# Layer 1 of a four-layer sequence model: attention weights turned by VectorE in 32x32 blocks, and weighed in array tiles of 32 rows by 64 columns

## The chip, the cores and the metric

The kernel runs on one core of a Trainium2 chip. The metric is device microseconds for one execution of the program, lower is better. Durations inside an execution come from one execution that the hardware profiler recorded; its times count from the first recorded instruction (the span).

## What is computed

Four layers act in turn on x, 8 sequences of 512 positions with 256 features, all in float32. Layers 0, 1 and 2 are transformer blocks (normalization, modulation by a condition vector, attention, a two-layer perceptron). Layer 3 is a bidirectional state-space layer. The change is in the attention of layer 1, which has 16 heads of 64 features:

```python
q, k, v = split(modulate(layernorm(x)) @ W_qkv)          # 16 heads of 64
attn = softmax(einsum('bqhd,bkhd->bhqk', q, k) * 64 ** -0.5)
out = einsum('bhqk,bkhd->bqhd', attn, v).reshape(B, T, 1024)
x = x + g_msa * (out @ W_out + b_out)
```

Layers 0 and 2 have 16 heads of 16 features. They form the transposed scores directly, so that their weights need no transposing.

## The kernel before, in words

**Layout and stages.** Activations lie with features on the partitions and the 512 positions along the free dimension. The three transformer layers are one program part: its list `units` holds one unit per batch for layers 0 and 2, and two per batch for layer 1 (`Cfg`, line 62; a unit is 8 heads), hence 8 + 16 + 8 units. The recurrence of layer 3 follows, in pools of its own. Its `fill` (line 1271) is of use here for its matmuls: 64 rows by 32 columns of the array, eight such tiles at a time, 128 moving columns each.

**Who sets the order.** All engines are on a manual schedule: each engine's instructions stand in the order in which the Python code emits them, and an engine starts an instruction only when all earlier ones on it have started. DMAs stand in order in SP's queue. Attention of layer 1 is `attend_q` (line 486). Its loop (line 548) runs over rounds. A round is two items of 128 queries for two heads, so four score tiles of 128 queries by 512 keys, and layer 1 has 128 rounds. In round r it emits:

1. `scores` of round r (line 494): four matmuls, two heads side by side in 64 rows of the array each, into four PSUM banks.
2. `weights` of round r (line 504): per tile a row maximum on VectorE (510) and an exponential on ScalarE that also sums its rows (511).
3. `weigh` of round r-2 (line 532): 16 matmuls of 128 columns, V as the stationary operand (128 keys by 64 features), two heads side by side in 64 columns of the array each; after four items a ScalarE copy of the finished output (545).
4. a share of the dense work (`dense.products`, line 333).
5. `turned` of round r-1 (line 522): per tile four TensorE transposes of 128x128 into a PSUM bank (529) and a VectorE copy of the bank to SBUF (530).
6. `divide` of round r (line 516): a reciprocal on VectorE (518) and one multiplication per tile on GpSimd (520).
7. a second share of dense work.

**Dense work.** `prep` (line 386) makes a unit's normalized input, Q, K and V, and must be done before the unit's first scores (`prepared`, 342). It waits in emission until the unit two before has been scored and weighed. `post` (line 680) makes the output projection and the perceptron of a batch. `products` hands out this work at `Q_RATE` units per round, in pieces that are not split, and lets a round go without when earlier pieces ran over. So the rounds are uneven: a piece can be 8 matmuls of 512 columns.

**Buffers.** PSUM has eight banks. Seven form a ring from which `bank()` (line 125) takes the next one; the eighth holds the output that `weigh` accumulates. The exponentials lie in four buffers of tag `p`, two rounds' worth. float32 matmuls appear in the profile as two records each (two passes), a transpose as one.

Of the kernel before, what the change touches and what calls it, by code (L numbers as in the profile page):

```python
# [7 lines left out]
F32 = mybir.dt.float32  # L8
# [10 lines left out]

LEAD, K_RATE, Q_RATE = 6, 3.7, 6.0  # L20
GELU = 4.0
# [27 lines left out]
class Cfg:  # L49
# [12 lines left out]
    Cfg(0, 16, 32, 1, 1e-5, AF.Gelu, (2, 0, None, 6, 4, None)),  # L62
    Cfg(1, 64, 64, 2, 1e-5, AF.Gelu, (0, 2, 4, 6, 8, 10)),
    Cfg(2, 16, 32, 1, 1e-6, AF.Gelu_apprx_tanh, (0, 2, 4, 6, 8, 10)),
# [10 lines left out]
def dit_mamba_kernel(ctx: ExitStack, tc: tile.TileContext, t, out):  # L75
# [44 lines left out]
    with ExitStack() as actx:  # L120
        apool = actx.enter_context(tc.tile_pool(name="apool", bufs=1))
        a2 = actx.enter_context(tc.tile_pool(name="a2", bufs=2))
        ps = actx.enter_context(tc.tile_pool(name="ps", bufs=1, space=PSUM))

        def bank():
            return ps.tile([128, L], F32, tag="s", name="s", bufs=7)

# [74 lines left out]
        def load_attn(cfg, g=0):  # L202
            l = cfg.layer
            src = t[f"wqkv{l}"].rearrange("(k p) m -> p k m", p=128)
            w = apool.tile([128, 2, 1536 if l == 1 else 768], F32, tag="wqkv", name="wqkv")
            if l == 1:

                for i in range(3):
                    o = i * 1024 + g * 512
                    nc.sync.dma_start(w[:, :, i * 512 : (i + 1) * 512], src[:, :, o : o + 512])  # L210
            else:
                for i in range(2):
                    pad = a2.tile([128, 2, L], F32, tag="p", name="pad", bufs=N_P)
                    nc.sync.dma_start(pad, src[:, :, i * 512 : (i + 1) * 512])
                    for k in range(2):
                        dst = w[:, k, i * 256 : (i + 1) * 256].rearrange("p (h r) -> p h r", r=16)
                        nc.gpsimd.tensor_copy(dst, real(pad[:, k, :]))
                nc.sync.dma_start(w[:, :, 512:768], src[:, :, 1024:1280])
                bv = apool.tile([128, D], F32, tag="bv", name="bv")
                nc.sync.dma_start(bv, t[f"bv{l}"].to_broadcast([128, D]))  # L220
                W["bv"] = bv
            W["qkv"] = w
# [55 lines left out]

        negp = [apool.tile([128, 4, 128], F32, tag=f"negp{i}", name="negp") for i in range(2)]
        clear(0, nc.vector)  # L280
        for i in range(2):
            nc.gpsimd.memset(negp[i], 0.0)
        load_x(0, 1)
        load_out(CFGS[0])

        class Unit:


            def __init__(self, idx, cfg, b, g):
                self.idx, self.cfg, self.b, self.g = idx, cfg, b, g  # L290
                self.i2 = idx % 2
                self.first = b == 0 and g == 0
                self.last = b == B - 1 and g == cfg.n_groups - 1
                self.ready = self.scored = self.weighed = False
                self.ot = {}
                self.qT, self.kT = qts[self.i2], kts[self.i2]
                self.v = vt[self.i2].rearrange("p (t h d) -> p t h d", t=4, d=cfg.pad)

# [87 lines left out]
        def prep(u):  # L386

            cfg, b, l = u.cfg, u.b, u.cfg.layer
            before = units[u.idx - 2] if u.idx > 1 else None
            load_x(l, b)  # L390
            if (l == 1 or u.first) and u.idx:
# [13 lines left out]
            if l == 1:  # L405
                for c in range(4):
                    p = plain(w, c * 128, h, 2)
                    nc.vector.tensor_scalar(u.qT[:, c, :], p, cfg.qscale, None, ALU.mult)
                    yield DONE
                    p = plain(w, 512 + c * 128, h, 2)  # L410
                    nc.scalar.copy(u.kT[:, c, :], p)
                    yield DONE
                while not before.weighed:
                    yield PASS
                for tt in range(4):
                    p = bank()
                    for k in range(2):
                        nc.tensor.matmul(
                            p, h[:, k, tt * 128 : (tt + 1) * 128], w[:, k, 1024:1536], start=k == 0, stop=k == 1
                        )  # L420
                    nc.scalar.copy(u.v[:, tt, :, :], p.rearrange("p (h d) -> p h d", d=64))
                    yield DONE
                u.ready = True
                return
            if l == 2:
                if b < 2:
                    while not before.weighed:
                        yield PASS
                    clear(u.i2, nc.gpsimd)
# [19 lines left out]
            for k in range(2):  # L449
# [12 lines left out]
                yield DONE  # L462
            while before and not before.weighed:
                yield PASS
# [21 lines left out]
        def attend_q(us):  # L486


            cfg = us[0].cfg
            nh = cfg.nh  # L490
            rounds = [(u, i) for u in us for i in range(0, 16, 2)]
            pr, pt, o = {}, {}, {}

# [10 lines left out]
            def weights(u, it, ss):  # L504
                c, qt = divmod(it, 4)
                p = pr[u, it] = a2.tile([128, 2, L], F32, tag="p", name="pr", bufs=N_P)
# [15 lines left out]
            def turned(u, it):  # L522
                d = pt[u, it] = [a2.tile([128, L], F32, tag=tag, name="pt") for tag in ("q2", "qks")]
                p = pr.pop((u, it))
                for j in range(2):
                    tp = bank()
                    for kt in range(4):
                        sl = slice(kt * 128, (kt + 1) * 128)
                        nc.tensor.transpose(tp[:, sl], p[:, j, sl], ident)  # L529
                    nc.vector.tensor_copy(d[j], tp)  # L530

            def weigh(u, it):
                c, qt = divmod(it, 4)
                if qt == 0:
                    o[c] = ps.tile([128, L], F32, tag="o", name="o")
                p = pt.pop((u, it))
                for kt in range(4):
                    for j in range(2):
                        nc.tensor.matmul(
                            o[c][rows(cfg, j), qt * 128 : (qt + 1) * 128], u.v[:, kt, c * 2 + j, :],  # L540
                            p[j][:, kt * 128 : (kt + 1) * 128], start=kt == 0, stop=kt == 3,
                        )
                if qt == 3:
                    u.ot[c] = out_tile()
                    nc.scalar.copy(u.ot[c], o[c])
                    u.weighed = c == 3

            for r in range(len(rounds) + 2):
                pend = []
                if r < len(rounds):  # L550
                    u, i = rounds[r]
                    if i == 0:
                        dense.prepared(u)
                    ss = [scores(u, i + k) for k in range(2)]
                    u.scored = i == 14
                    pend = [(u, i + k, weights(u, i + k, ss[k])) for k in range(2)]
                if r >= 2:
                    u, i = rounds[r - 2]
                    for k in range(2):
                        weigh(u, i + k)  # L560
                dense.products(Q_RATE / 2, 6, 2)
                if 1 <= r <= len(rounds):
                    u, i = rounds[r - 1]
                    for k in range(2):
                        turned(u, i + k)
                for args in pend:
                    divide(*args)
                dense.products(Q_RATE / 2, 6, 2)

        def attend_k(us):  # L570
# [26 lines left out]
            def extend(u, c):  # L597
                p = bank()
                for qt in range(4):
                    nc.tensor.transpose(p[:, qt * 128 : (qt + 1) * 128], negp[c % 2][:, qt, :], ident)  # L600
                q2[u, c] = a2.tile([128, L], F32, tag="q2", name="q2")
                nc.vector.tensor_tensor(q2[u, c], u.qT[:, c, :], p, ALU.add)

            def weigh(u, c, kt, pt):
                if kt == 0:
                    o[c] = ps.tile([128, L], F32, tag="o", name="o")
                for j in range(4):
# [9 lines left out]
                if c == 0:  # L617
                    u.s16 = a2.tile([16, L], F32, tag="s16", name="s16")
                if c % 2 == 0:
# [60 lines left out]
        def post(us):  # L680
# [9 lines left out]
            if l != 1:  # L690
# [3 lines left out]
                for qt in range(4):  # L694
                    nc.tensor.transpose(
                        p[:, qt * 16 : (qt + 1) * 16], u.s16[:, qt * 128 : (qt + 1) * 128], ident[0:16, 0:16]
                    )
                rec = a2.tile([128, 64], F32, tag="rec", name="rec")
                nc.vector.reciprocal(rec, p[:, 0:64])  # L699
                wide = apool.tile([128, 64, 16], F32, tag="wide", name="wide")  # L700
                nc.gpsimd.tensor_copy(wide, rec[:, :, None].to_broadcast([128, 64, 16]))  # L701
# [3 lines left out]
                for k in range(2):  # L705
                    p = bank()
                    for qt in range(4):
                        nc.tensor.transpose(
                            p[:, qt * 128 : (qt + 1) * 128], wide[:, qt, k * 128 : (k + 1) * 128], ident
                        )  # L710
                    nc.vector.tensor_tensor(u.ot[k], u.ot[k], p, ALU.mult)
                    yield 1
                yield PASS
# [853 lines left out]
```

## Time and profile before

| what | value |
| --- | --- |
| timed runs | 6252.9, 6258.54, 6271.06 us; median 6258.54 us |
| span of the profiled execution | 6255.0 us, mean granted clock 0.970; a time of its own besides the span is not recorded |
| layer 1's attention | first score matmul at 915.4 us, last weigh matmul ends at 2456.7 us |
| TensorE busy over the whole span | 5768.5 us (92%) |
| VectorE, ScalarE, GpSimd busy over the whole span | 4102.2, 3549.7, 3674.4 us |
| DMA | 260.34 MB, mean 42 GB/s |

The profile is read by stage: the shares of the whole span mix the attention layers with the recurrence, whose limits are others. "PE" is TensorE's matmuls, "PEld" its weight loads, "DVE" VectorE, "ACT" ScalarE, "POOL" GpSimd. In a group's row, busy is the time in which at least one of the group's instructions ran, and the mean is that of one instruction. Matmuls overlap, so that a matmul's mean is far longer than the distance from one start to the next. A merged row of the timeline gives a start, a length and a count: the length less one matmul's own duration, over the count less one, is that distance.

### The profile page before, as it was taken

To read this page: it belongs to the slowest core of one execution; us is meant where nothing else is said; L and a number is where in the kernel's file an instruction comes from. 1 tells how busy PE (TensorE), PEld (TensorE's weight loads), DVE (VectorE), ACT (ScalarE), POOL (GpSimd) and SP (SyncE) were. 2 spreads that over 40 slices of the span, in tenths; PEclk is the share of its full clock that TensorE was granted. 3 is DMA by queue.
4 is the path that set the end of the run, shared out by engine and by line. 5 is a ranking of instruction groups with operands and counts; after the bars stand their busy time and mean duration, and the time that the engine had idled before them with its cause. 6 is when DMAs were issued, how large, how long until landed. Compare 5 with 4: busy or idle time off the path is not lost. (4 is left out here: it accounts for less than half of the span.)

```text
span 6255.0 us, 200766 instructions
## 1 busy us (share of the span) xinstructions
PE 5768.5 (92%) x88988; PEld 2903.6 (46%) x88988; DVE 4102.2 (66%) x5109; ACT 3549.7 (57%) x6854; POOL 3674.4 (59%) x1467
## 2 busy tenths in 40 slices
PE   9999999999999998999998788898898988888887
PEld 4333335555555554333333444554455545444544
DVE  4555445444455544454552599888889888888887
ACT  2444443333344333344443677878777778777784
POOL 2010026555566565111110499999999989999897
PEclk8999999999999999999998899999999999999999
DMA  2000100000000000101000211212121111212120
GB/s 89 25 24 25 36 23 31 31 28 18 28 27 12 28 27 15 45 20 31 23 17 11 73 53 49 73 53 70 54 60 53 59 59 55 67 57 67 54 66 26
DMA packets 168913, 260.34 MB, mean 42 GB/s; under 512 B 40544, under 2 KB 58976, under 8 KB 168048
## 3 DMA queue, kind: packets, MB, share of 16 engines
q1 hardware_dynamic: 166992, 245.92, 12.9%
q8 instruction: 703, 11.52, 0.8%
q10 hardware_dynamic: 1056, 1.57, 0.1%
q14 instruction: 162, 1.33, 0.1%
HBM read 186.53 MB, written 34.60 MB: 35 GB/s over the span
## 5 line engine op out<-in xcount | busy, mean ns | idle before, releaser
L1297 POOL TENSOR_TENSOR hs<-hs,cs 128x2048 f32<-128x2048 f32 x512 | 2324.3, 4573 | 205.3 <-DVE hs L1293 131.8
L1293 DVE TENSOR_TENSOR_SCAN hs<-da,bx 128x512 f32<-128x512 f32 x2048 | 2303.0, 1197 | 201.8 <-PE bx L1279 130.7
L1254 ACT ACTIVATE da<-dtr,negA 128x512 f32<-128x512 f32 x2048 | 1394.5, 716 | 482.8 <-DVE hs L1293 471.4
L1279 PE MATMUL bx<-dg,ut 64*32 64x128 f32 x65536 | 1111.0, 273 | 183.5 <-DVE hs L1293 104.8
L1279 PEld LDWEIGHTS bx<-dg,ut 64*32 64x32 f32 x65536 | 925.3, 106 | 592.2 <-issue 449.7
L520 POOL TENSOR_SCALAR pr<-pr,sums 128x512 f32<-128x512 f32 x512 | 796.9, 1574 | 572.4 <-DVE sums L518 572.0
L593 DVE TENSOR_REDUCE negp<-s 128x1 f32<-128x512 f32 x1024 | 637.6, 683 | 590.4 <-PE s L588 590.0
L644 ACT ACTIVATE pt<-s 128x512 f32<-128x512 f32 x1024 | 528.0, 602 | 442.1 <-PE s L638 442.0
L1325 PE MATMUL yc<-hs,r 128*32 128x512 f32 x4096 | 573.7, 615 | 39.9 <-POOL hs L1297 39.8
L511 ACT ACTIVATE pr<-s,negm 128x512 f32<-128x512 f32 x512 | 345.1, 686 | 298.7 <-DVE negm L510 285.0
L530 DVE COPY pt<-s 128x512 f32<-128x512 f32 x512 | 322.0, 683 | 193.5 <-PE s L529 179.8
L510 DVE TENSOR_REDUCE negm<-s 128x1 f32<-128x512 f32 x512 | 317.3, 682 | 142.1 <-PE s L499 142.0
L588 PE MATMUL s<-kT,qT 32*128 32x512 f32 x2048 | 368.1, 654 | 36.2 <-ACT pt L644 18.2
L353 POOL TENSOR_TENSOR xs<-x 128x512 f32<-128x512 f32 x48 | 61.0, 1272 | 566.3 <-DVE x L664 187.4
L675 PE MATMUL s<-g,w_w 128*128 128x512 f32 x768 | 368.6, 627 | 23.9 <-ACT g L739 14.6
L1227 ACT ACTIVATE dg<-eye,bt 128x64 f32<-128x64 f32 x1528 | 381.5, 343 | 1.1 <-PE bx L1279 1.0
L701 POOL COPY wide<-rec 128x1024 f32<-128x1024 f32 x16 | 16.6, 1037 | 622.1 <-DVE rec L699 622.1
L381 PE MATMUL s<-h,w_w 128*128 128x512 f32 x768 | 364.0, 615 | 12.3 <-POOL h L372 12.3
L381 PE MATMUL s<-h,wqkv 128*128 128x512 f32 x768 | 366.1, 611 | 5.1 <-POOL h L372 5.1
L638 PE MATMUL s<-q,kT 32*128 32x512 f32 x2048 | 365.8, 649 | 1.9 <-DVE qs L455 1.4
L529 PE MATMUL s<-base,pr 128*128 128x128 f32 x2048 | 266.1, 281 | 43.6 <-POOL pr L520 38.5
L1325 PEld LDWEIGHTS yc<-hs,r 128*32 128x32 f32 x4096 | 122.6, 110 | 392.5 <-issue 261.2
(191 smaller groups left out, 6250.6 us busy)
## 6 DMA issues: line engine op xcount, KB each, us to landing
dtr<-dt_s SPq DMA_DIRECT2D x1024, 64.0 KB
cs<-c_s SPq DMA_DIRECT2D x256, 128.0 KB
wqkv<-in_wqkv_dram SPq DMA_DIRECT2D x48, 512.0 KB
dt_s<-dt SPq DMA_DIRECT2D x15, 1024.0 KB
x_mid<-x SPq DMA_DIRECT2D x24, 512.0 KB
x<-x_mid SPq DMA_DIRECT2D x24, 512.0 KB
ot<-ot SPq DMA_DIRECT2D x256, 32.0 KB
w<-in_w_in_dram SPq DMA_DIRECT2D x16, 512.0 KB
```

The source lines that it names most:

```text
L381: nc.tensor.matmul(p, w[:, k, o : o + 128], src[:, k, :], start=k == 0, stop=k == n - 1)
L520: nc.gpsimd.tensor_scalar(p[:, j, :], p[:, j, :], sums[:, j : j + 1], None, ALU.mult)
L588: nc.tensor.matmul(ss[j], u.qT[r, c, qt * 128 : (qt + 1) * 128], u.kT[r, c, :], start=True, stop=True)
L593: nc.vector.tensor_reduce(negp[c % 2][:, qt, i : i + 1], ss[j], AX.X, ALU.max, negate=True)
L644: nc.scalar.activation(pt[j // 2][:, j % 2, :], ss[j], AF.Exp)
L675: nc.tensor.matmul(p, w[:, first + c, m * 128 : (m + 1) * 128], srcs[c], start=c == 0, stop=c == n - 1)
L1227: nc.scalar.activation(o[:, n, :, i], eye, AF.Copy, scale=bt[:, 4 * i + n : 4 * i + n + 1])
L1254: nc.scalar.activation(da[:, i, :], dtr[step, 4 * c + j], AF.Exp, scale=negA[:, 4 * c + j, g : g + 1])
L1279: nc.tensor.matmul(bx[k][32 * n : 32 * n + 32, r, 128 * s : 128 * s + 128], uts[c][64 * r : 64 * r + 64, s, 32 * j : 32 * j + 32], d[64 * ...
L1293: nc.vector.tensor_tensor_scan(h, back(da[:, i, :]), back(x[:, i, :]), 0.0, ALU.mult, ALU.add)
L1297: nc.gpsimd.tensor_tensor(hs[t_], hs[t_], cs[step, k % 16 // 4][:, None, :, :].to_broadcast([128, 2, 2, L]), ALU.mult,)
L1325: nc.tensor.matmul(yc[c][32 * j : 32 * j + 32, :], r32, h[j // 2][:, j % 2, i, :], start=False, stop=gp == n_p - 1 and i == 1, tile_positi ...
```

## The change

Layer 1 is split into four units per batch, of four heads each (so 32 units), with `Q_RATE` 6.4 for 6.0. Its weights are turned in blocks of 32x32 on VectorE, straight from SBUF to SBUF. A block transpose of a tile of 128 queries by 512 keys leaves 32 keys on the partitions for each of the four groups of 32 queries, so each group of 32 partitions needs V of all keys. V is therefore written to DRAM once per unit, and read back four times, once into each group of 32 partitions. `weigh` then runs once for two heads and all 512 queries (64 times in all, in the odd rounds), as 128 matmuls of 32 rows by 64 columns with 128 moving columns, in eight array tiles, into four PSUM banks. All eight banks are now one ring (`s8`), from which `weigh` takes four neighbouring ones: the next four, or banks 0 to 3 if the next four would run over the end. Per unit two Q and two K products of 512 columns remain, and V is made in pieces of 256 columns. The buffers of the turned weights and of V's copies lie in Q, K and V tiles that layers 0 and 2 use; so at the turn to layer 2 its first unit waits, in emission, until layer 1's last unit has been scored, and clears its tiles on GpSimd after that. The turned weights' second pair of buffers waits for the division in the last batch of layer 0.

```diff
-LEAD, K_RATE, Q_RATE = 6, 3.7, 6.0
+LEAD, K_RATE, Q_RATE = 6, 3.7, 6.4
...
-    Cfg(1, 64, 64, 2, 1e-5, AF.Gelu, (0, 2, 4, 6, 8, 10)),
+    Cfg(1, 64, 64, 4, 1e-5, AF.Gelu, (0, 2, 4, 6, 8, 10)),
...
+        s8 = ps.tile([128, 8, L], F32, tag="s", name="s")
+        ring, n_ring = [0], [7]
         def bank():
-            return ps.tile([128, L], F32, tag="s", name="s", bufs=7)
+            i = ring[0] % n_ring[0]
+            ring[0] = i + 1
+            return s8[:, i, :]
+        def four_banks():
+            i = ring[0] % n_ring[0]
+            i = i if i <= 4 else 0
+            ring[0] = i + 4
+            return s8[:, i : i + 4, 0:128]
...
+        turned_t = [t_.rearrange("p (b q) -> p b q", q=128) for t_ in (extra, vt[1], aux, work)]
+        spread_t = [
+            t_.rearrange("p c t -> p (c t)").rearrange("p (b d) -> p b d", d=128) for t_ in (qts[1], kts[1])
+        ]
+        v_dram = [dram.tile([L, 256], F32, tag=f"vd{i}", name="v_dram") for i in range(2)]
...
+                nc.sync.dma_start(v_dram[u.i2].rearrange("(t p) d -> p t d", p=128), u.v)
                 u.ready = True
...
+            def spread_v():
+                while waiting and len(spread) < 2 and waiting[0][0].ready:
+                    u, c = waiting.pop(0)
+                    t_ = spread[u, c] = spread_t[c]
+                    for a in range(4):
+                        nc.sync.dma_start(
+                            t_[32 * a : 32 * a + 32, :, :],
+                            v_dram[u.i2][:, 128 * c : 128 * c + 128].rearrange("(b i) d -> i b d", i=32),
+                        )
...
             def turned(u, it):
-                d = pt[u, it] = [a2.tile([128, L], F32, tag=tag, name="pt") for tag in ("q2", "qks")]
+                c, qt = divmod(it, 4)
+                if qt == 0:
+                    heads[u, c] = [turned_t[(turns[0] + j) % 4] for j in range(2)]
+                    turns[0] += 2
+                    while turns[0] == 4 and not units[u.idx - 1].divided:
+                        dense.step(dense.posts)
                 p = pr.pop((u, it))
                 for j in range(2):
-                    tp = bank()
-                    for kt in range(4):
-                        sl = slice(kt * 128, (kt + 1) * 128)
-                        nc.tensor.transpose(tp[:, sl], p[:, j, sl], ident)
-                    nc.vector.tensor_copy(d[j], tp)
...
+                    nc.vector.transpose(heads[u, c][j][:, :, qt * 32 : qt * 32 + 32], p[:, j, :])
+            def weigh(u, c):
+                p, v, o = heads.pop((u, c)), spread[u, c], four_banks()
+                for b in range(16):
+                    for a in range(4):
+                        r = slice(32 * a, 32 * a + 32)
+                        for j in range(2):
+                            d = slice(64 * j, 64 * j + 64)
+                            nc.tensor.matmul(
+                                o[d, a, :], v[r, b, d], p[j][r, b, :], start=b == 0, stop=b == 15,
+                                tile_position=(32 * a, 64 * j),
+                            )
+                spread.pop((u, c))
...
```

## The prediction

> **What bounds the kernel now.** I read the table by stretch first, for the stage that the change touches: from the first score matmul of layer 1 to its last weigh.
>
> ```profile
> core 0: us, PE busy (x) PEld busy (x) DVE busy (x) ACT busy (x) POOL busy (x), PEclk, DMA share, GB/s
> 915.00:2457.00 1542.00, 1471.92 (x8799) 842.49 (x8796) 778.78 (x1450) 596.26 (x1352) 918.82 (x609) 0.97 0.07 25
> ```
>
> PE is busy 1472 of 1542 us; DVE 51%, ACT 39%, POOL 60%, DMA 7%. So PE's work sets the stage, 12.0 us for each of 128 rounds. Next the waits of PE in the same stretch, for the 70 us that are left, and the groups:
>
> ```profile
> PE s L529 <- POOL pr L520: 38.5, 49, 1.5
> PE s L675 <- DVE qs L455: 9.2, 1, 9.2
> ...
> PE s L529 <- ACT pr L511: 4.8, 3, 2.2
> ```
>
> ```profile
> L520 POOL TENSOR_SCALAR pr<-pr,sums 128x512 f32<-128x512 f32 x512 | 796.9, 1574 | 572.4 <-DVE sums L518 572.0
> ...
> L530 DVE COPY pt<-s 128x512 f32<-128x512 f32 x512 | 322.0, 683 | 193.5 <-PE s L529 179.8 <-PE o L539 9.4 <-DMA qT<-qs 2.2
> L510 DVE TENSOR_REDUCE negm<-s 128x1 f32<-128x512 f32 x512 | 317.3, 682 | 142.1 <-PE s L499 142.0
> L529 PE MATMUL s<-base,pr 128*128 128x128 f32 x2048 | 266.1, 281 | 43.6 <-POOL pr L520 38.5 <-ACT pr L511 4.8
> ...
> L539 PE MATMUL o<-pt,vt 128*64 128x128 f32 x4096 | 253.6, 276 | 1.2 <-DVE pt L530 1.2
> ```
>
> Most of PE's idle time stands in front of the transposes (L529), which the change removes. L539's row counts 4096: 2048 matmuls in two passes. Last, merged rows of the timeline, for what a matmul costs PE, which its mean does not tell:
>
> ```profile
> 1506.47 1.99 PE L499 MATMUL s<-kT,qT 64*128 64x512 f32 x8
> 1508.03 2.48 DVE L510 TENSOR_REDUCE negm<-s 128x1 f32<-128x512 f32 x4
> 1508.39 1.97 PE L539 MATMUL o<-pt,vt 128*64 128x128 f32 x32
> 1517.26 1.91 PE L529 MATMUL s<-base,pr 128*128 128x128 f32 x16
> ```
>
> ```profile
> 2490.55 1.14 PE L638 MATMUL s<-q,kT 32*128 32x512 f32 x8
> ```
>
> ```profile
> 3534.34 2.03 PE L1279 MATMUL bx<-dg,ut 64*32 64x128 f32 x128
> ```
>
> From start to start a transpose costs (1.91 - 0.28)/15 = 109 ns, a weigh record (1.97 - 0.28)/31 = 54.5 ns: two column tiles share 109 ns. The L1279 row is of the recurrence: eight tiles of 64x32, also 128 columns, (2.03 - 0.27)/127 = 13.9 ns each, so eight share 111 ns. L638 shows four tiles of 32 rows at once: 8 records of 512 columns in 1.14 us, where one after the other takes 3.4 us (8 x 429 ns, the distance of 512-column records in L499's stretch).
>
> **The change part by part.** The sum is made against the profiled span, 6255.0 us, which lies 3.5 us below the median of the three timed runs; I add the 3.5 at the end.
>
> 1. *The transposes leave PE.* A round's 16 hold it for 1.81 us (from 1501.13 to the next product's start at 1502.94): 128 x 1.81 = 232 us off the path. With them goes the wait in front of them, 38.5 + 4.8 us, and L539's 1.2: 44 us. What is late next is treated in 5 and 6.
>
> 2. *Weigh in 32x64 tiles.* 8192 matmuls, 16384 records. No row shows a 32x64 tile. Upper bound on speed is L1279's 13.9 ns: 228 us, against 4096 x 54.5 = 223 us before. The lower bound is that only two tiles run side by side, as in L539: 54.5 ns, 893 us. I take 13.9, since L1279 shows eight tiles and L638 four row groups, and the number of weight columns loaded per row group in 109 ns (two times 64) is that of L539. It shows one weak point: later in such a burst starts are 16.7 ns apart for stretches, and these bursts are 256 records long, not 128; at 16.7 throughout it is 46 us more. Start-up of the bursts falls from 128 to 64. I book 0.
>
> [...] The trace has 13.9 ns from start to start with eight tiles. [...] I go by the row.
>
> 3. *V in pieces.* Its 256-column records are 231 ns apart where they stand already (L470), the 512-column ones 447 ns (L418): 512 x 231 - 256 x 447 = +4 us. Q and K keep their number of columns.
>
> 4. *V through DRAM.* Per unit one write of 512 KB and eight reads of 256 KB, 512 packets of 512 bytes each. Around 1509 us a write and a load of 512 KB with 2048-byte packets took 4.8 us together, 92 ns a packet over 16 engines; at that price a pair's four reads take 2048 x 92/16 = 12 us. A copy of V is freed by one weigh and needed by the next but one, four rounds or some 40 us later. So the rounds hide it; uncovered it would cost up to 12 us 64 times. In SP's queue only wqkv loads and x transfers stand behind these reads, of which each has rounds of slack; the DMA share rises from 7% to about half.
>
> 5. *DVE turns.* 512 copies of 683 ns go, 512 block transposes come. Bounds: a plain SBUF pass of DVE is 1277 ns for 2048 elements (L273), so 320 ns for 512; the slowest pass of 512 elements is the scan at 1197 ns (L1293). I take 683, the row of the same element count that is replaced. DVE then does as much as before, 779 us, and stays under PE; at 1197 it does 1042. [...]
>
> But the order on DVE now decides when weigh may start: the transposes of round r-1 stand behind the four reductions of round r. Where an even round has no dense work, PE comes to the next weigh after two score groups (1.92 us each from 1506.47 to 1508.39), at 3.8 us. DVE needs 1.1 us until the first scores, 2.48 for the reductions and four times 0.68 for the transposes, 6.3 with a semaphore: 2.5 us of new wait. Counted in the order of the changed program, 20 of 64 even rounds have less than 3 us of PE work: 20 x 2.5 = 50 us. An even round with two or three products (5 us) hides it. Behind the waiting weigh stands PE's dense work, and behind that, on DVE, the evictions, then the reciprocals for POOL's division. At 1197 ns this rises by 20 x 2.05 = 41 us.
>
> 6. *One ring of eight banks.* In 17 weighs the four neighbouring banks overlap those just scored (six with one tile, six with two, five with three). They wait for that tile's exponential, about 1.0, 1.7 or 2.4 us after the scores' end (exponentials 0.67 us apart from 1508.81): 28 us.
>
> 7. *POOL.* Its divisions stay, 4 x 1.57 = 6.3 us a round; between the last one of a round and the next one's first stand one transpose and a reciprocal, about 1 us. With the normalizations (0.9 us a round) POOL needs 8.2 us a round, under the 10.5 forecast below. It does not bound, but is the nearest.
>
> 8. *The ends.* At the turn to layer 2, POOL clears three tiles after the last scores (1.8 + 1.8 + 5.4 + 1.8 us), behind six us of division; DVE's evictions of Q wait for the mask's scaling behind that, and the last transposes and the last weigh stand behind those. About 12 us of PE waiting, but before has its own there (9.2 us in the waits above, some 20 us idle from 2380 to 2457). I book 0, with 20 us for the range. The recurrence and layer 0 keep their instructions.
>
> Sum for the stage: PE's work 1472 - 232 + 4 = 1244; waits 70 - 44 = 26 that stay, 50 and 28 new: 1348 us, 194 less than 1542. 6255 - 194 + 3.5 = **6065 us**.
>
> **The rivals.**
>
> *A, the forecast.* PE still bounds, 6065. Without parts 5's and 6's waits it gives 5987; that is the low end.
>
> *B, the turning is dear and the tiles run at 16.7 ns.* For: no row shows either. The stage loses 41 + 46 us more, and up to 20 at the turn: 6065 + 107 = 6172. Still faster.
>
> *C, the wait only moves.* Weigh waits in every odd round, not in 20: for DVE's transposes or for V, 3 us each. 64 x 3 = 192 us takes the gain: about 6257, no change. Against: an ordinary even round has 7 us of PE work, and V 40 us of time. It needs a V read above 40 us.
>
> *D, slower: the tiles don't run eight at a time.* The place is weigh's 128 matmuls. At L539's 54.5 ns the weighing is 893 us, 665 more: 6065 + 665 = 6730. It decides the sign from (228 + 194)/16384 = 25.8 ns per record. Against: both tile rows above. For: rows and columns at these sizes together are in no row, nor is accumulation over 16 steps in four banks at once.
>
> **How the numbers follow.** A 0.63, B 0.23, C 0.06, D 0.08. A difference under 0.3% (19 us) is about what a measurement of this kernel can't tell from none. Faster is A and B with a little of C, 0.87; same the rest of C, 0.05; slower D, 0.08. The range takes A and B whole, 5985 to 6175, and leaves out C and D, 0.14; the ends stand close to the bounds, hence 8 in 10.
>
> **What would show it.** PE records in the stage fall from 2048 + 4096 to 16384 in a weigh group whose bursts of 256 last 3.6 to 4.3 us (right) or 14 (D). The block transpose's mean tells 5: near 0.68, or 1.2 (B). PE's waits should name DVE's transposes and ACT's exponentials in front of weigh, some 80 us together, not DMA (C). The stage should be about 1350 us, and the time after it unchanged within 20. Wrong would be: a POOL above 90% busy in the stage, a POOL division slower than 1.57 us because DVE now works in SBUF beside it, or a lower granted clock.

## The result, and the profile after

The changed kernel takes 6364.93 us (median of 4 runs, 6346.51 to 6369.54), the kernel before 6263.49 us beside it (4 runs). The ratio is 1.0156, 95% interval [1.0138, 1.0174]: slower by 1.6%, where 3% faster was forecast. The profiled execution took 6346.51 us (span 6344.7) and is the fastest of the four, so that the spans show 90 us of a difference of 101.

The 90 us by stage, from the starts and ends of the matmuls of layers 1 and 2:

| stage | before | after | difference |
| --- | --- | --- | --- |
| up to the first score of layer 1 | 915.4 us | 919.7 us | +4.3 |
| layer 1, first score to last weigh | 1541.4 us | 1596.6 us | +55.2 |
| from there to the last weigh of layer 2 | 888.1 us | 918.5 us | +30.4 |
| the rest (recurrence) | 2910.2 us | 2909.9 us | -0.3 |

The table by stretch of the changed kernel, for layer 1's stage:

```profile
core 0: us, PE busy (x) PEld busy (x) DVE busy (x) ACT busy (x) POOL busy (x), PEclk, DMA share, GB/s
920.00:2516.00 1596.00, 1347.57 (x19303) 746.52 (x19300) 776.47 (x1451) 601.81 (x1352) 908.66 (x605) 0.93 0.31 78
```

PE's busy time fell from 1472 to 1348 us, and yet the stage grew: PE now stands still for 248 us of it, where it was 70. The granted clock went from 0.97 to 0.93. The groups of this stretch say what the new instructions cost:

```profile
L574 POOL TENSOR_SCALAR pr<-pr,sums 128x512 f32<-128x512 f32 x512 | 792.6, 1567 | 596.9 <-DVE sums L572 596.9
...
L594 PE MATMUL s<-aux,kT 32*64 32x128 f32 x4096 | 177.5, 311 | 83.1 <-issue 37.6 <-ACT pr L565 22.7 <-DVE aux L585 20.9
L594 PE MATMUL s<-work,kT 32*64 32x128 f32 x4095 | 173.3, 311 | 23.3 <-issue 20.4 <-DVE sums L572 0.8
L594 PE MATMUL s<-extra,qT 32*64 32x128 f32 x4096 | 158.0, 296 | 44.6 <-issue 30.2 <-ACT vt L458 10.4 <-ACT pr L565 3.4
L594 PE MATMUL s<-vt,qT 32*64 32x128 f32 x4096 | 156.4, 297 | 24.8 <-issue 23.7
```

```profile
L585 DVE STREAM_TRANSPOSE aux<-pr 128x512 f32<-128x512 f32 x128 | 88.1, 689 | 10.0 <-POOL pr L574 10.0
...
L585 DVE STREAM_TRANSPOSE work<-pr 128x512 f32<-128x512 f32 x128 | 86.6, 676 | 12.3 <-POOL pr L574 12.3
```

The block transpose (L585) takes 0.68 us, as booked, and POOL's division is no slower. The weigh matmuls (L594) are 16384 records, and in front of all four groups stands "issue": PE was idle and waited for nothing that the profile shows. The waits of PE in the stretch, with the total, the count and the longest, put that first:

```profile
engine line waited for: us in total, times, longest us
PE s L594 <- issue: 111.9, 69, 4.6
PE s L397 <- POOL ss L393: 35.4, 7, 6.3
PE s L594 <- ACT pr L565: 26.1, 33, 2.2
PE s L594 <- DVE aux L585: 20.9, 1, 20.9
PE s L412 <- POOL h L403: 18.4, 4, 4.7
PE s L594 <- ACT vt L458: 10.4, 3, 3.5
```

The names in this list are inferred, and for waits in front of a burst's first matmul they mislead. These lines of the timeline (1356.0 to 1356.86 us) show why:

```profile
1356.08 0.67 DVE L585 STREAM_TRANSPOSE extra<-pr 128x512 f32<-128x512 f32 x1
...
1356.85 0.29 PE L594 MATMUL s<-extra,qT 32*64 32x128 f32 x1 [1.56 <-issue]
```

The matmul reads `extra` and starts 0.10 us after the end of a block transpose that writes it. So do the first matmuls of 22 of the 64 bursts, after waits of 37 us in sum, which the list has under "issue" (21.5 us), ScalarE's exponentials (15 us) and a step of the normalization on ScalarE. Together with the 20.9 us in front of the last weigh, weigh waits 58 us for its turned weights. The other 90 us of "issue", 56 waits, stand inside bursts, and so do 11 us of waits for exponentials. The 90 us are the subject of what follows.

From first to last start, the 64 bursts of weigh last 440 us in sum, 6.9 us each, where 3.6 was forecast. One of them shows why. The table by stretch of L594's own instructions, before, in and after the pause of the burst that starts at 1908.11 us:

```profile
core 0: us, PE busy (x) PEld busy (x), PEclk, DMA share, GB/s
1908.11:1911.02 2.91, 2.76 (x152) 2.52 (x154) 1.00 1.17 242
1911.30:1915.84 4.54, 0.00 (x0) 0.00 (x0) 0.82 0.42 75
1915.84:1918.00 2.16, 2.16 (x81) 2.16 (x88) 0.50 0.04 8
```

After 152 matmuls nothing runs for 4.5 us, and what follows runs at half the clock (granted 0.50, 81 matmuls in 2.16 us). The DMA view of the first part of that pause, 1911.02 to 1913.37 us (busy tenths of the 16 engines, then the queues: packets, MB, share):

```profile
DMA  9999999999999999999999997968745445343300
...
q1 hardware_dynamic: 823, 0.41, 93.8%
```

and of 1913.38 to 1914.46 us:

```profile
q8 instruction: 1, 0.02, 6.1%
q1 hardware_dynamic: 1, 0.00, 0.1%
```

First the DMA engines are full of V's copies (q1, the packets of 512 bytes). As these drain, one packet of instructions (q8) goes through, from 1913.39 to 1914.45 us; 1.40 us later PE goes on:

```profile
1915.84 0.37 PE L594 MATMUL s<-aux,kT 32*64 32x128 f32 x1 [4.55 <-issue]
```

This is no single case. Of the 76 pauses above 0.6 us within bursts (132 us, counted from start to start), 49 (93 us, median 1.6 us) end 1.25 to 1.5 us after an instruction packet, and six more (13 us) lie just outside these bounds; the other 21 (27 us) are waits for exponentials, for ScalarE's copy of V out of PSUM, and for DVE. All 56 waits for "issue" inside bursts end 1.20 to 1.55 us after a packet. Counting all such pauses above 0.3 us (58, ending 1.20 to 1.56 us after a packet), the number of matmuls of any kind from one pause to the next is 253, 381, 253, 254, 382, 254, 252, 1015, ...: for all 57 distances a multiple of 127 to within three matmuls, and that multiple is each time the number of packets between. So a packet feeds about 127 matmuls with their 127 weight loads. The total agrees: 152 packets and 38966 TensorE instructions in the stage (71 and 18151 in the kernel before), 256 for each. The page of the changed kernel gives a packet's size: 784 packets hold 12.85 MB, 16.4 KB each, or, an estimate from the two counts, 64 bytes for each of some 256 instructions.

```profile
q8 instruction: 784, 12.85, 0.9%
```

A weigh's 256 matmul records are 512 TensorE instructions, two packets. At 13.9 ns per record PE uses up a packet in 1.8 us. A packet takes 1.1 us (median), and PE resumes some 1.4 us after it: 2.4 us from the packet's start (median over the 58 pauses, 2.2 to 3.2), and more when it starts late. Counted in these units of 127, the transfer of a packet starts when PE, by the matmuls that have ended, is 0 to 150 matmuls ahead of the first one that needs it (median 91), so no more than about a packet and a fifth ahead. In the kernel before a weigh was 32 records, between scores and dense products whose instructions last far longer (429 ns from start to start, median of the dense records of 512 columns, for 54.5 in a weigh), and the trace shows no such pause in its stage, not one above 0.6 us that ends 1.25 to 1.5 us after an instruction packet. In its recurrence there are such pauses, in the bursts of L1279. The waits of PE in the whole kernel before have:

```profile
PE bx L1279 <- issue: 74.4, 92, 2.5
```

Of these 92 waits, 85 (70 us) end 1.20 to 1.55 us after an instruction packet, and all distances between the 85 are multiples of 127 matmuls to within two. So the trace before already held this wait, in the row from which the prediction took its 13.9 ns.

### The profile page after: what moved, and what is told of

It is laid out like the page before. It is cut to its first block, busy times and chain, and to the rows that moved or that the text cites. A ratio compares the mean times of both kernels' runs of the same rounds, so it can differ in the third digit from the quotient of the medians.

```text
span 6344.7 us, 221568 instructions
## 1 busy us (share of the span) xinstructions
PE 5652.4 (89%) x99484; PEld 2820.4 (44%) x99484; DVE 4100.7 (65%) x5109; ACT 3553.9 (56%) x6854; POOL 3670.3 (58%) x1467
## 3 DMA queue, kind: packets, MB, share of 16 engines
q8 instruction: 784, 12.85, 0.9%
q10 hardware_dynamic: 1056, 1.57, 0.1%
## 5 line engine op out<-in xcount | busy, mean ns | idle before, releaser
L654 DVE TENSOR_REDUCE aux<-s 128x1 f32<-128x512 f32 x1024 | 637.5, 683 | 612.6 <-PE s L649 612.4
L649 PE MATMUL s<-kT,qT 32*128 32x512 f32 x2048 | 373.4, 660 | 54.3 <-ACT pt L705 23.9
L762 POOL COPY aux<-rec 128x1024 f32<-128x1024 f32 x16 | 16.6, 1037 | 670.4 <-DVE rec L760 670.4
L699 PE MATMUL s<-work,kT 32*128 32x512 f32 x2048 | 373.8, 653 | 13.7 <-DVE qs L495 13.7
L669 PE MATMUL s<-pt,vt 128*32 128x512 f32 x2048 | 280.2, 618 | 1.0 <-ACT ot L676 1.0
L554 PE MATMUL s<-kT,qT 64*128 64x512 f32 x1024 | 261.1, 632 | 0.0
```

What stands on the lines that cost most here:

```text
L649: nc.tensor.matmul(ss[j], u.qT[r, c, qt * 128 : (qt + 1) * 128], u.kT[r, c, :], start=True, stop=True)
L654: nc.vector.tensor_reduce(negp[c % 2][:, qt, i : i + 1], ss[j], AX.X, ALU.max, negate=True)
L699: nc.tensor.matmul(ss[j], u.kT[r, c, i * 128 : (i + 1) * 128], q2[u, c][r, :], start=True, stop=True)
```

## The experiments

Two theories went into the runs. Both take the names of the wait list at their word. **Theory I**: the bursts outrun the loading of instructions, and V's packets delay that loading further. **Rival II**: weigh waits for its turned weights and banks on DVE and ScalarE, and the pauses only show where these waits would. A third has V's traffic alone as the cause. Each run was timed beside the kernel before on the same chip: 6260.53 us for split, V once, aligned and the four units, 6261.20 for late and the last three rows, 6259.79 for the rest.

| run | us (median) | ratio to before, 95% interval | layer 1's stage | layer 2 |
| --- | --- | --- | --- | --- |
| the changed kernel | 6364.93 | 1.0156 [1.0138, 1.0174] | 1596.6 | 918.5 |
| split | 6297.90 | 1.0061 [1.0046, 1.0076] | 1531.4 | 928.2 |
| V once | 6330.74 | 1.0109 [1.0089, 1.0128] | 1572.9 | 920.7 |
| aligned | 6347.33 | 1.0143 [1.0127, 1.0158] | 1600.5 | 914.7 |
| four units in the kernel before | 6306.04 | 1.0074 [1.0058, 1.0089] | 1571.4 | 898.7 |
| late | 6312.48 | 1.0085 [1.0064, 1.0107] | 1537.9 | 923.1 |
| late and split | 6268.46 | 1.0013 [1.0003, 1.0022] | 1502.4 | 927.7 |
| ... with longer pauses of normalization | 6320.02 | 1.0093 [1.0078, 1.0108] | 1547.9 | 929.4 |
| around | 6282.74 | 1.0035 [1.0022, 1.0048] | 1515.1 | 924.7 |
| turn | 6345.12 | 1.0132 [1.0115, 1.0149] | 1588.1 | 923.8 |
| late, split and turn | 6247.27 | 0.9981 [0.9970, 0.9992] | 1483.8 | 924.4 |
| ... in four pieces | 6260.74 | 1.0001 [0.9990, 1.0012] | 1490.6 | 922.0 |
| ... with more dense work per round | 6264.32 | 1.0008 [0.9997, 1.0020] | 1497.6 | 927.6 |

**Split.** One dense step between the two halves of a weigh; the work is the same.

```diff
                 for b in range(16):
+                    if b in (8,):
+                        dense.done += dense.product(2)
                     for a in range(4):
```

> The changed kernel with one step of dense work between the first eight and the last eight key blocks of each weigh; everything is still computed. Theory I (instructions): a weigh is 512 TensorE instructions, two packets of 16 KB, and TensorE uses up a packet in 1.8 us while the next takes about 3 us to come; a product of 1.75 us between the halves gives the fetch its time, the pauses inside weigh (93 us that end 1.2 to 1.5 us after an instruction packet) fall to under 40 us, and the time falls from 6365 to 6285 to 6320 us. Rival II (operands): the pauses are waits for the transposes, the exponentials or V; then they stay and the time stays within 15 us of 6365.

Measured: 6297.90 us, 67 us less than the changed kernel. The waits of PE in its stage:

```profile
PE s L596 <- issue: 54.8, 33, 4.0
PE s L596 <- DVE aux L585: 23.2, 1, 23.2
PE s L596 <- ACT pr L565: 23.0, 29, 1.8
```

"Issue" has halved. Inside bursts it fell from 90 to 25 us, and the pauses that end behind an instruction packet from 49 (93 us) to 12 (24 us). The waits that end with a block transpose, counted as above and with the turn, rose from 59 to 92 us, those inside bursts with them, since PE comes to them earlier. Only one dense step has moved between the halves, so the pauses inside bursts are the loading of instructions, as theory I has it. Rival II is wrong on the pauses; the waits that it names exist beside them.

**V once.** V is read back for the first unit only.

```diff
-                    for a in range(4):
+                    for a in range(4 if u is us[0] else 0):
```

> The changed kernel, in which V is read back from DRAM for the first unit of layer 1 only; later units weigh with the first unit's V, so the result of layer 1 is not the reference's. 248 of 256 reads of 256 KB go. Theory I (instructions) with a fetch that is slow by itself: the pauses of 1.3 to 2 us inside weigh stay and only the nine above 2.5 us shrink, 10 to 25 us off 6365. Rival III (V's packets hold the instruction packets up): all pauses inside weigh go, 80 us or more off 6365.

Measured: 6330.74 us, 34 us less than the changed kernel, between the two expectations. The stage's DMA share fell from 0.31 to 0.12, instruction-packet pauses from 49 (93 us) to 35 (69 us), those above 2.5 us from nine to six. Its waits:

```profile
PE s L594 <- issue: 74.0, 44, 4.1
PE s L594 <- DVE aux L585: 47.9, 15, 20.7
...
PE s L594 <- DVE extra L585: 10.3, 7, 1.6
```

Most of the pauses stay without V's packets, so these don't make them; the median of a pause stays at 1.6 to 1.7 us, and long ones remain, up to 4.1 us idle, at this DMA share of 0.12 (53864 packets of q1 in the stage, 1044 bytes each on average). This list puts DVE's name to the waits in front of the bursts, 58 us in 22 places. They are not new: without the 20.7 us at the turn they are 37 us in 21 places, as much as the changed kernel has under other names.

**Aligned.** A jump of the ring, so that a weigh never takes banks that were just scored.

```diff
                     spread_v()
+                    if r >= 2 and rounds[r - 2][1] % 4 == 2 and ring[0] % 8 in (1, 2, 3):
+                        ring[0] = 4
                     ss = [scores(u, i + k) for k in range(2)]
```

> The changed kernel; ahead of the scores of a round with a weigh the bank counter jumps to 4 where it stood at 1, 2 or 3, so that weigh's four banks are never among those just scored. The waits of weigh for ScalarE (26 us behind exponentials, 10 us behind V's copy) fall under 10 us and the time falls by 15 to 40 us; the pauses behind instruction packets stay at 80 to 110 us. If weigh's waits were all for instructions, nothing changes.

Measured: 6347.33 us, 18 us less by the medians, but the two ratios' intervals overlap, and the profiled stage is no shorter (1600.5 us), so a gain in time is not shown. The waits for exponentials inside bursts, 11 us before, are gone: the six that the list still has end 0.1 us behind block transposes. The 10 us behind ScalarE's copy of V stayed, against the expectation. "Issue" grew by 13 us:

```profile
PE s L594 <- issue: 124.8, 73, 4.8
...
PE s L594 <- ACT pr L565: 11.1, 6, 1.8
```

**Four units in the kernel before.** The kernel before with nothing but the split of a batch into four units of four heads, and `Q_RATE` 6.4.

```diff
-LEAD, K_RATE, Q_RATE = 6, 3.7, 6.0
+LEAD, K_RATE, Q_RATE = 6, 3.7, 6.4
...
-    Cfg(1, 64, 64, 2, 1e-5, AF.Gelu, (0, 2, 4, 6, 8, 10)),
+    Cfg(1, 64, 64, 4, 1e-5, AF.Gelu, (0, 2, 4, 6, 8, 10)),
```

> The kernel before with the split alone: four units of four heads per batch in layer 1 and 6.4 units of dense work a round, with the TensorE transposes, the old weighing and no V through DRAM. If the split is cheap: 6250 to 6285 us, that is within 20 us of before. If the split (reloading weights 32 times, smaller V pieces, uneven rounds) costs what the change lost: 6300 us or more.

Measured: 6306.04 us, 46 us more than the kernel before, as the second expectation had it, though less than half of what the change lost. In the profiled execution, 43 us longer than that of the kernel before, 30 lie in layer 1's stage (PE busy 1486 us for 1472, idle 85 for 70) and 11 in layer 2. Its waits of PE:

```profile
PE s L537 <- POOL pr L528: 36.0, 53, 0.9
PE s L384 <- POOL h L375: 20.7, 10, 4.6
```

The wait for POOL's normalization (h) was 3.8 us in the kernel before. Smaller units give each preparation less time; that this is the reason was not tested. This part of the change the prediction had not priced at all.

**Late, and late with split.** The weigh stands behind the first share of dense work, first with the split, later by itself.

```diff
+                dense.products(Q_RATE / 2, 6, 2)
                 if r >= 2:
                     u, i = rounds[r - 2]
                     if i % 4 == 2:
                         weigh(u, i // 4)
                         spread_v()
-                dense.products(Q_RATE / 2, 6, 2)
```

> The weigh of an even round is issued behind the first share of dense work instead of in front of it, and its two halves again have one dense step between them. Theory I (a weigh of 512 small TensorE instructions outruns the loading of instructions; waits for DVE and ACT are the smaller part): the split alone brought 6298; standing later, the weigh no longer waits for ScalarE's exponential in overlapping banks (26 us in the changed kernel), but its output leaves later: 6275 to 6295. Rival II (weigh waits for the turned weights and their banks, and the pauses only stand where those waits would): late alone takes the waits away, at most 47 us of them, and the split adds nothing: 6315 to 6335 with the pauses back.

> The changed kernel with one edit: the weigh of an even round stands behind the first share of dense work, in one burst of 256 matmuls. The run with this and the split took 6268. Theory I (the loading of instructions makes the pauses): the burst has its 512 instructions as before and its pauses stay near 112 us; what falls is the 26 us of waiting for ScalarE in overlapping banks, and the dense work in front lets more of the burst's first packets arrive: 6315 to 6345. Rival II (the pauses are the wait for turned weights and banks, which the dense work now hides): 6265 to 6285, as with the split, which then adds nothing.

Measured: 6268.46 us together, 7 us below the range of theory I, and 6312.48 for late alone. Late alone is 3 us below the range of theory I, and 27 above that of rival II in its second expectation; its waits:

```profile
PE s L594 <- issue: 99.4, 65, 4.1
PE s L412 <- POOL h L403: 57.3, 11, 8.5
...
PE s L594 <- ACT pr L565: 11.6, 14, 1.8
```

The pauses stayed (44 behind an instruction packet, 77 us; 92 us of waits for instructions inside bursts, for 90). What fell is the wait for turned weights, from 58 us in front of bursts, the turn with them, to 10. The exponentials' own waits inside bursts stayed at 9 us, for 11, so the reason in theory I's expectation was wrong: late takes away what rival II names, and leaves what theory I names. So the two edits work on different things: 44 us of the gain of late and split is the split's.

**Longer pauses of normalization.** Late and split, with five planner passes instead of two behind each of POOL's later steps.

```diff
-            yield from passes(2)
+            yield from passes(5)
...
-            yield from passes(2)
+            yield from passes(5)
```

> As the run with the weigh later and split, and the two later pauses of a normalization last five planner passes instead of two, so that POOL has its sums and its scaled rows done when PE comes. PE's waits for the normalization (35 and 18 us in the changed kernel) should fall by 20 to 40 us. If POOL's order, not PE's early arrival, is what is late, the waits move to the unit's first product or to the scores and the time stays within 10 us of the run without it.

Measured: 6320.02 us, 52 us more than late and split, outside both expectations. The idea was wrong:

```profile
PE s L596 <- issue: 56.5, 28, 8.9
PE s L387 <- POOL xs L384: 46.9, 9, 8.9
PE s L596 <- ACT pr L565: 45.0, 26, 6.1
PE s L412 <- POOL h L403: 33.0, 6, 7.5
```

Probably a preparation that starts its steps later is forced through at the end, where PE waits for its first sum (xs); the wait for exponentials (45 us) is not explained by that.

**Around.** The first eight key blocks of a weigh in front of the first share of dense work, the last eight behind it, with the aligned banks. While a weigh is open, its four banks are left out of the ring.

```diff
-                        weigh(u, i // 4)
-                        spread_v()
+                        w = weigh(u, i // 4)
+                        next(w)
                 dense.products(Q_RATE / 2, 6, 2)
+                if r >= 2 and i0 % 4 == 2:
+                    next(w, None)
+                    spread_v()
```

> Each weigh's first eight key blocks stand in front of the first share of dense work, the last eight behind it, and the banks are chosen so that a weigh never takes those just scored. Theory I: more matmuls of 512 columns stand between the halves than the one step of the split run, so that the pauses are as short or shorter, and the wait for ScalarE falls from 26 us to about 11: 6265 to 6290. Where the even round has no dense work between, the pause comes back. Rival (the halves cost more starts of bursts, and the output's later eviction holds back the banks): 6300 to 6320.

Measured: 6282.74 us, within the expectation of theory I, but not for its reason: "issue" inside bursts is 41 us, more than with the plain split (25), and PE waits 70 us for h. No wait for exponentials is left; the 24 us under their name end behind block transposes.

**Turn.** In the changed kernel, only the turn to layer 2: DVE clears the first tiles, and layer 2's first preparation waits for layer 1's last unit to be weighed.

```diff
-                    clear(u.i2, nc.gpsimd)
+                    clear(u.i2, nc.gpsimd if b else nc.vector)
...
-            while before and not before.scored:
+            while before and not (before.weighed if turn and not b else before.scored):
...
+                while l == 1 and not units[us[-1].idx + 1].ready:
+                    dense.product(2)
```

> Only the turn to layer 2 is changed, in the changed kernel: DVE clears the first two tiles instead of POOL, and layer 2's first preparation waits for the last unit weighed, so that it doesn't stand in front of the last round's work; the weigh is not split. If the turn's 30 us (layer 2's start, 918 against 888) come from the clears and preparations that stand in POOL's queue in front of the last weigh: 6325 to 6345, with the stage of layer 1 about 20 shorter. If they come from dense work that the smaller units leave over, the time stays at 6355 to 6370.

Measured: 6345.12 us, 20 us less by the medians. The wait of the last weigh for DVE (20.9 us) is gone from the profile, but the ratios' intervals overlap, and the profiled stage is only 8.5 us shorter, with more "issue" (129.5 us). The next run settles it. Layer 2 itself did not get shorter (923.8 us).

**Late, split and turn; four pieces; more dense work.** The three edits that helped, together; then with pieces of four key blocks; then with `Q_RATE` 7.0.

```diff
-                    if b in (8,):
+                    if b in (4, 8, 12):
```

```diff
-LEAD, K_RATE, Q_RATE = 6, 3.7, 6.4
+LEAD, K_RATE, Q_RATE = 6, 3.7, 7.0
```

> The weigh later and split, and the turn to layer 2 mended as in the run of the turn alone (20 us there). If the two are independent: 6268 - 20 = 6248, with 6240 to 6258; that is 0 to 0.3% under the kernel before. If the wait at the turn was only what the pauses left over, 6260 to 6270.

> As the run with the weigh later and split and the turn mended, but a weigh in four pieces of four key blocks, 128 instructions each, with a dense step between each two. Theory I: the 22 us of pauses that were left with two pieces fall under 10, and the starts and ends of 128 more bursts cost about the same, 0.1 us each: within 10 us of the two pieces, 6235 to 6260. If starts of bursts cost more than the pauses that are left, or the dense steps give out and POOL's normalizations come late: 6260 to 6285.

> As the run with the weigh later and split and the turn mended, with the share of dense work per round raised from 6.4 to 7.0, so that preparations run earlier. If PE's waits for the normalization (47 us for h with the weigh late and split) come from preparations that start too late: 10 to 25 us faster than at 6.4. If the dense work then gives out before each round's end, so that more rounds have nothing between a weigh's halves, the pauses come back: 5 to 30 us slower.

Measured: 6247.27, 6260.74 and 6264.32 us. The first is under the kernel before by 0.19%, with an interval of 0.08% to 0.30%, and 21 us under late and split, their intervals apart: the turn's 20 us are real, as the first expectation had it. Its stage:

```profile
core 0: us, PE busy (x) PEld busy (x) DVE busy (x) ACT busy (x) POOL busy (x), PEclk, DMA share, GB/s
921.00:2405.00 1484.00, 1314.48 (x19277) 720.95 (x19273) 767.38 (x1448) 598.86 (x1350) 897.91 (x600) 0.93 0.33 83
```

```profile
PE s L412 <- POOL h L403: 41.1, 11, 5.8
PE s L596 <- issue: 31.4, 16, 9.1
PE s L596 <- ACT pr L565: 19.7, 17, 1.8
PE s L412 <- DMA wqkv<-in_wqkv_dram: 19.1, 10, 7.9
```

Of this, 19 us of "issue" are the loading of instructions. The block transposes now cost more than that: some 48 us of waits end with one, 9 of them in front of the last weigh, under the names of "issue", ScalarE and DVE.

Four pieces leave as much "issue" as two (31.9 us) and cost 13 us more by the medians, with intervals that just touch, and just past the range for theory I: the pauses that were left (19 us, 13 with four pieces) are not worth more starts. More dense work per round gave 17 us back, with "issue" at 44.6 us, as the second expectation had it.

## Why the prediction was wrong, point by point

**1, the transposes leave PE: right.** Their rows and the wait in front of them are gone, and PE's busy time fell by 124 us.

**2, weigh in small tiles: this step failed.** The distance was right: 149 matmuls in the 2.15 us from 1647.14 us are 14.4 ns each, and all distances under 100 ns at full clock average 14.1. What failed is "I book 0" for bursts of 256 records. The term was 228 us and measured 440, 212 more: 132 us of pauses above 0.6 us, 93 of them tied to an instruction packet as above, and about 48 from the half clock, at which some 3450 of the records were started. The last 32 are shorter stops, most of them at the starts of bursts. The row of the recurrence that the price came from has bursts of half that length, 128 records or one packet of instructions. Even these stop for packets, 70 us over the recurrence; the price was read from one burst that did not, and the wait list that shows it was read for layer 1's stage alone. I saw longer bursts as the weak point, and looked for it in 16.7 for 13.9 ns.

**3, V in pieces: right, but not the whole.** Without idle time, 512 columns of V take 449 ns from start to start in two pieces, 442 in one, which is 2 us over all, where 4 were booked. What was left out is the split into four units, which alone costs 46 us.

**4, V through DRAM: half right.** PE waits for V nowhere among the rows of the changed kernel. But its packets stand in the way of the instructions': without them 34 us go. The price was too high, 37 ns a packet for 92, and the DMA share is 0.31, not "about half".

**5, DVE's turning: right.** 0.68 us as taken, and the wait in front of weigh came: 37 us in 22 bursts, for 50 in 20. The profile has it under other names.

**6, the ring: too large.** The waits for exponentials in overlapping banks are 11 us, for 28. The 26 us of the list come near 28 by chance: 15 of them are waits for block transposes. Another 10 us stand behind ScalarE's copy of V, which the prediction had not counted.

**7, POOL: right on the division** (1.57 us, 57% busy in the stage), but not on what else hangs on POOL: PE waits 54 us for its normalizations (the rows ss and h), where it was 13 before (xs, h and ss).

**8, the ends: too small.** One wait of 20.9 us in front of the last weigh, and 30 us more in layer 2 (PE busy 872 us for 860, idle 47 for 28). The turn run and its combination show 20 us for the queue of clears and preparations; layer 2's 30 us stayed in every variant of the changed kernel, 27 to 41 us, and of these 11 come with the four units. The rest is open.

**The clock** stood in the prediction's last sentence, and came: time lost to the half clock in the stage rose from 39 to 111 us. Its 46 stretches last 3.4 us (32 of them), 6.8 (13) and 23.9 (one), and in the 3.4 us ahead of them PE was busy for 26% on average, and for up to 62%, against 84% over the stage (32% and 95% in the kernel before). But late, split and turn, with few pauses left, still loses 104 us (a granted clock of 0.93 over 1484 us). Which of the smaller waits cause that is open.

In sum for the stage: PE busy 1348 for 1244, of which the clock explains some 59 (182 us of the busy time fell to the half clock, 64 before); idle 248 for 104, of which 90 are the loading of instructions, 59 the block transposes with the turn, 54 POOL's normalizations and 21 ScalarE's exponentials and copies of V. **The rivals:** B's causes didn't come, D's neither (eight tiles do run at once, 14.1 ns from start to start). C has the right idea, a wait that takes the place of the one removed, but DVE held up 22 bursts and not 64, the reads of V none, and the wait that took the gain is for the instructions themselves.

In the best version, 58 us of the 194 remain in layer 1's stage (1483.8 for 1541.4), and layer 2 gives 36 back.

## What to carry to other kernels

Count instructions as a stream that has to be loaded: when matmuls become so small that 256 instructions run in less time than the next 16 KB of them take to arrive (here 1.8 us against some 2.4), price each packet at the difference, and mix in long instructions (a split with one dense step between was worth 67 us here). Traffic that nobody waits for isn't free while such a stream is loading beside it: without V's packets the kernel here was 34 us shorter. A name that a profile infers for a wait is worth a check against the ends of the instructions around it: here 37 us of waits for one engine stood under two other names. And a change that alters the size of a unit of work has to be priced by itself, before the edit that it is meant to serve.

## What the runs showed of the hardware that was not expected

TensorE stops in long bursts of small matmuls for want of instructions, in units of 127 matmuls with their weight loads, and the pause ends 1.2 to 1.56 us after the end of a 16 KB packet. The packet itself takes 1.1 us, and its transfer started at most some 150 matmuls ahead of need. While V's 512-byte packets filled the DMA engines (93.8% in the first part of the longest pause), pauses grew to 4.8 us; in V once, at a DMA share of 0.12, PE still stood idle for up to 4.1 us. Eight tiles of 32 rows by 64 columns sustain 14.1 ns from start to start with 128 moving columns, where eight of 64 by 32 have 14.0 (L1279 of the kernel before, all distances under 100 ns at full clock). A float32 block transpose of 128x512 on VectorE takes 0.66 to 0.72 us (medians 0.67 to 0.70), about as much as the copy of that size out of PSUM in the kernel before (0.67 to 0.69, median 0.68).
